# A fourth bank for picks, sums beside the constants, and pair steps two apart, in a graph edge kernel

## Chip, cores and metric

The kernel runs on one core of a Trainium2 chip. The metric is the device time of one execution, in microseconds (us). Engines are named as in the profile: PE (TensorE, matrix products), PEld (its weight loads), DVE (VectorE), ACT (ScalarE), POOL (GpSimd), SP (SyncE, here the queue that issues most transfers). PSUM is the memory that PE writes to; in this kernel it is cut into eight banks of 512 float32 numbers in each of 128 partitions.

## The reference

A layer of a graph network, 6250 nodes, 100000 edges and 128 features. For each edge the features of both ends and of the edge go through one matrix, a layer norm and a ReLU; the results are added up by source node; the node's own features are added and normalised.

```
msg_in = concatenate([x[row], x[col], edge_attr], axis=-1)   # 100000 x 384
h = msg_in @ W + b                                           # W: 384 x 128
mu, var = mean(h), mean(square(h - mu))                      # over 128 features
h = (h - mu) * rsqrt(var + 1e-5) * gamma + beta
msg = relu(h)
agg = segment_sum(msg, row, num_segments=6250)
out = layernorm(x + agg)                                     # eps 1e-5
```

Edges arrive sorted by `dst` (the column), not by `row`, so the sum over `row` needs a sort.

## The kernel before

**Three stages over the edges.** First the products of nodes with their part of W are made and cut into three bfloat16 terms (`project`, during the first split); those of the source nodes stay in SBUF as `xa`. Then a loop over 196 values of q takes four tiles of 128 edges at a time: `edge_loads` and `edge_window` fetch, `edge_hot` makes a one-hot matrix (DVE, L607), `edges` adds the edge's own product (PE, L619) and the destination node's row (PE, L623) in a bank `hp`, `evict` copies the bank out (ACT, L633), and `scatters` writes each row by an indirect transfer (POOL, L650) to its place in a table in DRAM, sorted by blocks of 125 source nodes. A row's place comes from `places`, a generator which for every piece of up to 44 tiles makes one-hots against an iota row (DVE, L451), runs a prefix sum (L455), counts (PE, L467 and L468; DVE, L470 to L472), multiplies (L474) and adds the 50 blocks up on PE (L502), a number `PG` of blocks side by side, which a reduction (DVE, L507) folds.

The tiles come in six splits, each with its own table. Once a split is written, its 25 pairs of blocks are worked on while the next split's edges go through the loop. That is the **pair stage**: 125 pairs of the first five splits, with eight tiles each (three splits), six or four. Pairs of eight or six tiles have two groups, of four or three tiles; pairs of four have one. The 25 pairs of the sixth split come in a tail, as 14 `Unit`s of one or two pairs, with their own lines (L847 to L958), among them sums (L912), which take turns between a bank `hp` and the bank of the sums.

**The steps of a pair** (class `Pair`), each in the program's order of its engine:

| step | engine, line | what it does |
|---|---|---|
| load | SP, L724 | a pair's rows from DRAM to `hl` |
| ones | DVE, L742 | one-hot of the row's node in its block, against the iota row in PSUM |
| turn, turned | PE, L754; ACT, L758 | transpose to a bank `tr`, copy out to `ohn` |
| seed(g) | ACT, L764 | rows of a group to a bank `sel` |
| pick(g) | PE, L781 | adds the source nodes' rows to them, three terms for each tile |
| square(g) | ACT, L790, L793 | sums of squares, standard deviation |
| root(g), scale(g) | DVE, L799, L805 | reciprocal, scaled and clipped row to `msg` |
| sums | PE, L814 | adds messages by node, in a bank `pa` |
| add | DVE, L819 | adds that to `acc` |

`FLOW` is a list of (step number, function), walked from the top once for each step of `work`; a pair starts a new round every four steps, so steps whose numbers are equal modulo four fall together, of pairs one or more apart. `due` and `steps_due` spread the steps over q: 100 steps over 42, 42, 30, 20 and 16 values of q, while the next split is written. One step comes between `edges` and `evict`, the others behind the scatters and the steps of `places`. From q = 13 on each q's scatters are tied to PE products through `done`.

**Banks before:** two `hp`, three `sel`, one `tr`, one `pa` and one `beside`. The last holds the iota row (`iota_p`, columns 0 to 127), a zero (`zero_p`), a piece's places so far (`at`), and from column 192 on `counts`: the counts, the 50 block sums of `places` (`PG` = 7 blocks of up to 44 columns), the flags' sum and, in the tail, the row `beta_p` that `stats` (L930) reads. The framework adds the waits between engines by the tiles and banks that the instructions touch.

Of the kernel before, what the change touches and what calls it, by code (L numbers as in the profile page):

```python
# [8 lines left out]
F32 = mybir.dt.float32  # L9
BF16 = mybir.dt.bfloat16  # L10
# [6 lines left out]
P = 128  # L17
D = 128
# [6 lines left out]
NB, BN = 50, 125  # L25
# [6 lines left out]
PIECES = 196  # L32
TABLE_FROM = [0, 13, 45, PIECES]
HALF = PIECES // 2
BANKS = {"hp": 2, "sel": 3, "tr": 1}


SPLITS = [(168, 4, 320, [12, 24, 44, 44, 44]),
# [7 lines left out]
BY_PE = 4  # L46
FN = 4

PG = 7
PG_AT = 192  # L50
XG = 4
ROW = 132
ACW = 130
# [31 lines left out]
def fast_path(ctx, tc, io, bad_d, found):  # L85
# [88 lines left out]
    iota_i = const.tile([P, P], I32, name="iota_i")  # L174
# [12 lines left out]
    beside, counts = beside_t[:, :PG_AT], beside_t[:, PG_AT:]  # L187
    iota_p, zero_p, at = beside[:, 0:P], beside[:, P:P + 1], beside[:, P + 8:P + 8 + NB]
# [10 lines left out]
    over_w = const.tile([P, 2], F32, name="over_w")  # L199

    def constants():
        nc.vector.tensor_copy(iota_p, iota_i)
# [48 lines left out]
    def signs():  # L251
        nc.vector.tensor_scalar(gamma_r, gamma_r, 0.0, 2.0, op0=ALU.is_ge, op1=ALU.mult)
        nc.vector.tensor_scalar(sgn_r, gamma_r, -1.0, None, op0=ALU.add)
        spread = psum.tile([P, 512], F32, name="pa")[:, :D]
        nc.tensor.matmul(spread, ones_h[0:1, :], sgn_r, start=True, stop=True)
        nc.scalar.copy(sgn, spread)

# [115 lines left out]
    n_banks = 0  # L373
# [5 lines left out]
    def project(g, k):  # L379
# [4 lines left out]
        t0 = g * XG  # L384
        m = XG if k == 1 else min(XG, NB - t0)
        xT = xT_of[g, k % 2]
        name = ("sel", "sel", "tr", "sel")[n_banks % 4]
# [340 lines left out]
    class Pair:  # L728
# [78 lines left out]

        def sums(self):
            k = self.k
            pa_t = psum.tile([P, 512], F32, name="pa")  # L810
            self.pa = pa_t[:, :2 * ACW].rearrange("p (h d) -> p h d", h=2)
            for h in range(2):
                for j in range(h, k, 2):
                    pe(nc.tensor.matmul(self.pa[:, h, :], self.ohe[:, j, :], self.msg[:, j, :],  # L814
                                        start=(j == h), stop=(j == k - 2 + h)), 4)
# [12 lines left out]
    class Unit:  # L828
# [73 lines left out]
        def sums(self, g):  # L902
            if (self.p0 + g) % 2:
                pa_t = psum.tile([P, PT, P], F32, name="hp", bufs=BANKS["hp"])
                pa = flat(pa_t)
            else:
                pa = psum.tile([P, 512], F32, name="pa")
# [91 lines left out]
    first, second = pieces[0][1], pieces[1][1]  # L999
# [72 lines left out]
    FLOW = [(14, second(lambda x: x.add())), (11, second(lambda x: (x.root(1), x.scale(1)))),  # L1072
            (13, single(lambda x: x.add())),
            (9, lambda x: (x.root(0), x.scale(0))), (13, second(lambda x: x.sums())),
            (8, second(lambda x: x.pick(1))), (6, second(lambda x: x.pick(0))),
            (5, single(lambda x: x.pick(0))),
            (7, second(lambda x: x.seed(1))), (5, second(lambda x: x.seed(0))),
            (3, single(lambda x: (x.turned(), x.seed(0)))),
            (9, second(lambda x: x.square(1))), (7, lambda x: x.square(0)),
            (4, second(lambda x: x.turned())), (2, lambda x: x.turn()),  # L1080
            (10, single(lambda x: x.sums())),
            (0, lambda x: x.ones()),
            (-6, None)]

# [428 lines left out]
```

## Time and profile before

| | |
|---|---|
| median of 3 runs | 1356.2 us (1353.18 to 1357.1) |
| the profiled execution's own time | 1355.95 us |
| its span in the trace | 1354.1 us |
| mean granted TensorE clock | 0.855 of full |
| busy: PE, PEld, DVE | 978.5, 869.8, 852.2 us |
| busy: ACT, POOL | 766.6, 799.0 us |

A row of the groups gives the line, engine, operation and tiles, count, then busy time and mean duration of one in ns, and at last the idle time just before them with the releasers. A row of the waits reads: engine and line that waited, what it waited for, us in total, times, longest. "issue" is time in which nothing that the profile shows was waited for; "remote" is a semaphore whose sender the profile can't tell. A row of the timeline gives start and duration in us.

### The profile page before, as it was taken

The numbers are of one execution on the slowest core, as the hardware profiler recorded it, in microseconds if no ns is written. First come the engines' busy times: TensorE is split into PE (matmuls) and PEld (weight loads), VectorE is DVE, ScalarE is ACT, GpSimd is POOL, SyncE is SP. The second block draws the span as 40 slices with busy tenths as digits, with TensorE's granted clock in tenths as the row PEclk, the third lists the DMA queues.
The fourth block names the chain that finished last, engine by engine and source line by source line (L and its number), as shares of the span: only waits on it lengthen the run. The fifth ranks groups of instructions, "written<-read, shape, count | busy, mean of one in ns | idle before, by whom it ended". The sixth has DMA issues, their size and how long they took to land. (4 is left out here: it accounts for less than half of the span.)

```text
span 1354.1 us, 27281 instructions
## 1 busy us (share of the span) xinstructions
PE 978.5 (72%) x8886; PEld 869.8 (64%) x8886; DVE 852.2 (63%) x2376; ACT 766.6 (57%) x2988; POOL 799.0 (59%) x830
## 2 busy tenths in 40 slices
PE   7555546365768777777877778778878787776895
PEld 5454535344757766676666767777778787665674
DVE  8572425514665666656575667678688877654797
ACT  4223322112656655565555567677779788755796
POOL 3656666666666665666566666656665556556054
PEclk9768687666888887888888798989999999988998
DMA  7857677445666654556756555666667655543332
GB/s 225 251 172 243 191 229 223 138 155 167 192 204 208 203 160 162 166 181 193 219 177 195 174 191 180 218 199 191 188 200 235 189 186 188 158 147 99 108 126 70
DMA packets 128050, 247.20 MB, mean 183 GB/s; under 512 B 47005, under 2 KB 61231, under 8 KB 127897
## 3 DMA queue, kind: packets, MB, share of 16 engines
q1 hardware_dynamic: 101924, 191.92, 46.8%
q0 software_dynamic: 25104, 53.05, 11.1%
q8 instruction: 71, 1.16, 0.4%
q14 instruction: 81, 0.66, 0.1%
q10 hardware_dynamic: 870, 0.40, 0.1%
HBM read 155.49 MB, written 89.80 MB: 181 GB/s over the span
## 5 line engine op out<-in xcount | busy, mean ns | idle before, releaser
L650 POOL DMA_INDIRECT sorted<-hs,place_i x782 | 760.6, 973 | 474.7 <-issue 179.7
L781 PE MATMUL sel<-xa,ohn 128*128 128x128 bf16 x2550 | 210.8, 232 | 134.7 <-issue 65.5
L790 ACT ACTIVATE sq<-sel 128x128 f32<-128x128 f32 x850 | 224.5, 281 | 140.4 <-remote 47.2
L619 PE MATMUL hp<-w,eT 128*128 128x128 f32 x1564 | 261.2, 316 | 32.4 <-issue 20.5
L814 PE MATMUL pa<-msg,ohe 128*128 128x130 f32 x1700 | 259.0, 307 | 30.0 <-DVE msg L805 14.9
L619 PEld LDWEIGHTS hp<-w,eT 128*128 128x128 f32 x1564 | 235.0, 226 | 67.2 <-issue 32.9
L781 PEld LDWEIGHTS <-ohn 128*128 128x128 bf16 x2550 | 175.0, 104 | 154.4 <-issue 136.1
L633 ACT COPY hs<-hp 128x512 f32<-128x512 f32 x196 | 114.2, 584 | 273.9 <-remote 98.5
L814 PEld LDWEIGHTS pa<-msg,ohe 128*128 128x128 f32 x1700 | 234.8, 216 | 41.5 <-issue 24.2
L805 DVE SCALAR_TENSOR_TENSOR msg<-sel,rstd,cut 128x128 f32<-128x128 f32 x850 | 240.7, 346 | 8.0
L790 ACT ACTIVATION_READ_ACCUMULATOR sq<-sel 128x1 f32 x850 | 179.8, 212 | 0.0
L819 DVE TENSOR_TENSOR acc<-acc,pa 128x260 f32<-128x260 f32 x125 | 52.9, 423 | 184.7 <-remote 72.8
L742 DVE TENSOR_TENSOR ohe<-hl,beside 128x1024 f32<-128x1024 f32 (+2 forms) x125 | 131.6, 1053 | 24.2 <-remote 7.6
L758 ACT COPY ohn<-tr 128x1024 bf16<-128x1024 bf16 (+2 forms) x125 | 109.6, 877 | 42.8 <-remote 19.2
L764 ACT COPY sel<-hl 128x512 f32<-128x512 f32 (+1 forms) x225 | 128.5, 571 | 2.0 <-DVE msg L805 2.0
L607 DVE TENSOR_SCALAR ohd<-db,part_w 128x512 bf16<-128x512 bf16 x192 | 68.6, 357 | 68.4 <-remote 36.8
L623 PE MATMUL hp<-win,ohd 126*128 126x128 bf16 x782 | 90.5, 238 | 15.9 <-issue 13.3
L799 DVE RECIPROCAL rstd<-std 128x4 f32<-128x4 f32 (+1 forms) x225 | 38.7, 172 | 90.3 <-ACT std L793 45.2
L754 PE MATMUL tr<-ident_h,ohe 128*128 128x128 bf16 x850 | 77.0, 229 | 21.9 <-issue 19.9
L623 PEld LDWEIGHTS <-ohd 126*128 126x128 bf16 x782 | 69.5, 109 | 23.3 <-issue 18.9
L754 PEld LDWEIGHTS <-ohe 128*128 128x128 bf16 x850 | 57.7, 103 | 29.9 <-issue 29.9
L793 ACT ACTIVATE std<-ss,eps 128x4 f32<-128x4 f32 (+1 forms) x225 | 67.1, 298 | 7.3
(198 smaller groups left out, 1018.9 us busy)
## 6 DMA issues: line engine op xcount, KB each, us to landing
eT<-in_eT SPq DMA_DIRECT2D x96, 512.0 KB
hl<-sorted SPq DMA_DIRECT2D x75, 528.0 KB
db<-drel_d SPq DMA_DIRECT2D x96, 256.0 KB
sorted<-empty SPq DMA_DIRECT2D x100, 198.0 KB
hl<-sorted SPq DMA_DIRECT2D x50, 264.0 KB
sorted<-hs,place_i POOLq DMA_INDIRECT x782
hl<-sorted SPq DMA_DIRECT2D x25, 396.0 KB
sorted<-empty SPq DMA_DIRECT2D x50, 132.0 KB
```

The costliest lines, as they stand in the source:

```text
L619: pe(nc.tensor.matmul(hp[:, j, :], eT[:, at], w[:, 2, :], start=j == 0, stop=False, skip_group_check=True), 4)
L623: pe(nc.tensor.matmul(hp[:, j, :], oh[:3 * WN, at], win[:3 * WN, :], start=False, stop=j == m - 1, skip_group_check=True))
L633: nc.scalar.copy(hs[:, :m, 0:D], hp[:, :m, :])
L650: i = nc.gpsimd.indirect_dma_start(out=sorted_d[s][:, :], out_offset=bass.IndirectOffsetOnAxis(ap=place_i[:parts, t:t + 1], axis=0), in_=h ...
L742: nc.vector.tensor_tensor(self.ohe[:, :k, :], self.hl[:, :k, D:D + 1].to_broadcast([P, k, P]), row_bc(iota_p, k), op=ALU.is_equal)
L754: pe(nc.tensor.transpose(tr[:, j, :], half[:, j0 + j, 1::2], ident_h))
L758: nc.scalar.copy(self.ohn[:, :self.k, :], self.tr[:, :self.k, :])
L764: nc.scalar.copy(self.sel[g][:, :m, :], self.hl[:, j0:j0 + m, 0:D])
L781: pe(nc.tensor.matmul(sel[:, j, :], self.ohn[:, j0 + j, :], xa[:, b, i * D:(i + 1) * D], start=False, stop=j == m - 1 and i == 2, skip_gro ...
L790: nc.scalar.activation(sq[:, j, :], self.sel[g][:, j, :], AF.Square, accum_out=ss[:, j:j + 1])
L805: nc.vector.scalar_tensor_tensor(self.msg[:, j0 + j, 0:D], self.sel[g][:, j, :], rstd[:, j:j + 1], cut, op0=ALU.mult, op1=ALU.max)
L814: pe(nc.tensor.matmul(self.pa[:, h, :], self.ohe[:, j, :], self.msg[:, j, :], start=(j == h), stop=(j == k - 2 + h)), 4)
```

## The change

`BANKS["sel"]` goes from 3 to 4. The bank `pa` is gone: the pair's sums, those of even pairs in the tail and the spread of signs at the start go to columns 252 to 511 of the bank `beside`, named `sums_p`. To make room there, the iota row is kept as bfloat16 in 64 columns (made through a bfloat16 tile `iota_h` in SBUF), `counts` begins at column 120 and has 132 columns, and `PG` goes from 7 to 3. The projections of the start take turns among five banks. In `FLOW`, for pairs with two groups, seeds go from 5 and 7 to 4 and 5, pick 1 from 8 to 7, squares from 7 and 9 to 8 and 9, scale 0 from 9 to 10, the add from 14 to 15; for pairs with one group, only the sums move, from 10 to 11.

```
--- before.py
+++ after.py
@@ -32,7 +32,7 @@
 PIECES = 196
 TABLE_FROM = [0, 13, 45, PIECES]
 HALF = PIECES // 2
-BANKS = {"hp": 2, "sel": 3, "tr": 1}
+BANKS = {"hp": 2, "sel": 4, "tr": 1}
 
 
 SPLITS = [(168, 4, 320, [12, 24, 44, 44, 44]),
@@ -46,8 +46,9 @@
 BY_PE = 4
 FN = 4
 
-PG = 7
-PG_AT = 192
+PG = 3
+PG_AT = 120
+PA_AT = 252
 XG = 4
 ROW = 132
 ACW = 130
@@ -184,8 +185,10 @@
     iota_row = const.tile([P, P], F32, name="iota_row")
 
     beside_t = psum.tile([P, 512], F32, name="beside")
-    beside, counts = beside_t[:, :PG_AT], beside_t[:, PG_AT:]
-    iota_p, zero_p, at = beside[:, 0:P], beside[:, P:P + 1], beside[:, P + 8:P + 8 + NB]
+    counts, sums_p = beside_t[:, PG_AT:PA_AT], beside_t[:, PA_AT:]
+    iota_w, zero_p, at = beside_t[:, 0:P // 2], beside_t[:, P // 2:P // 2 + 1], beside_t[:, 68:68 + NB]
+    iota_p = iota_w.bitcast(BF16)
+    iota_h = const.tile([P, P], BF16, name="iota_h")
     part = const.tile([P, 1], F32, name="part")
     before = const.tile([P, P], BF16, name="before")
     ident_h = const.tile([P, P], BF16, name="ident_h")
@@ -199,7 +202,8 @@
     over_w = const.tile([P, 2], F32, name="over_w")
 
     def constants():
-        nc.vector.tensor_copy(iota_p, iota_i)
+        nc.vector.tensor_copy(iota_h, iota_i)
+        nc.vector.tensor_copy(iota_w, iota_h.bitcast(F32))
         nc.vector.tensor_copy(iota_row, iota_i)
         nc.vector.tensor_copy(part, part_i)
         nc.vector.memset(zero_p, 0.0)
@@ -251,7 +255,7 @@
     def signs():
         nc.vector.tensor_scalar(gamma_r, gamma_r, 0.0, 2.0, op0=ALU.is_ge, op1=ALU.mult)
         nc.vector.tensor_scalar(sgn_r, gamma_r, -1.0, None, op0=ALU.add)
-        spread = psum.tile([P, 512], F32, name="pa")[:, :D]
+        spread = sums_p[:, :D]
         nc.tensor.matmul(spread, ones_h[0:1, :], sgn_r, start=True, stop=True)
         nc.scalar.copy(sgn, spread)
 
@@ -384,7 +388,7 @@
         t0 = g * XG
         m = XG if k == 1 else min(XG, NB - t0)
         xT = xT_of[g, k % 2]
-        name = ("sel", "sel", "tr", "sel")[n_banks % 4]
+        name = ("sel", "sel", "tr", "sel", "sel")[n_banks % 5]
         n_banks += 1
         ps = psum.tile([P, XG, P], F32, name=name, bufs=BANKS[name])
         for j in range(m):
@@ -807,8 +811,7 @@
 
         def sums(self):
             k = self.k
-            pa_t = psum.tile([P, 512], F32, name="pa")
-            self.pa = pa_t[:, :2 * ACW].rearrange("p (h d) -> p h d", h=2)
+            self.pa = sums_p.rearrange("p (h d) -> p h d", h=2)
             for h in range(2):
                 for j in range(h, k, 2):
                     pe(nc.tensor.matmul(self.pa[:, h, :], self.ohe[:, j, :], self.msg[:, j, :],
@@ -904,7 +907,7 @@
                 pa_t = psum.tile([P, PT, P], F32, name="hp", bufs=BANKS["hp"])
                 pa = flat(pa_t)
             else:
-                pa = psum.tile([P, 512], F32, name="pa")
+                pa = sums_p
             pa = pa[:, :2 * ACW].rearrange("p (h d) -> p h d", h=2)
             for h in range(2):
                 for j in range(h, self.kp, 2):
@@ -1069,16 +1072,18 @@
     def single(step):
         return lambda x: step(x) if len(x.groups) == 1 else None
 
-    FLOW = [(14, second(lambda x: x.add())), (11, second(lambda x: (x.root(1), x.scale(1)))),
+    FLOW = [(15, second(lambda x: x.add())), (11, second(lambda x: (x.root(1), x.scale(1)))),
             (13, single(lambda x: x.add())),
-            (9, lambda x: (x.root(0), x.scale(0))), (13, second(lambda x: x.sums())),
-            (8, second(lambda x: x.pick(1))), (6, second(lambda x: x.pick(0))),
+            (9, single(lambda x: (x.root(0), x.scale(0)))),
+            (10, second(lambda x: (x.root(0), x.scale(0)))), (13, second(lambda x: x.sums())),
+            (7, second(lambda x: x.pick(1))), (6, second(lambda x: x.pick(0))),
             (5, single(lambda x: x.pick(0))),
-            (7, second(lambda x: x.seed(1))), (5, second(lambda x: x.seed(0))),
+            (5, second(lambda x: x.seed(1))), (4, second(lambda x: x.seed(0))),
             (3, single(lambda x: (x.turned(), x.seed(0)))),
-            (9, second(lambda x: x.square(1))), (7, lambda x: x.square(0)),
+            (9, second(lambda x: x.square(1))), (8, second(lambda x: x.square(0))),
+            (7, single(lambda x: x.square(0))),
             (4, second(lambda x: x.turned())), (2, lambda x: x.turn()),
-            (10, single(lambda x: x.sums())),
+            (11, single(lambda x: x.sums())),
             (0, lambda x: x.ones()),
             (-6, None)]
```

More of the change, by code (lines that the diff above doesn't have):

```diff
@@ L34 @@
 HALF = PIECES // 2
-BANKS = {"hp": 2, "sel": 3, "tr": 1}
+BANKS = {"hp": 2, "sel": 4, "tr": 1}
 SPLITS = [(168, 4, 320, [12, 24, 44, 44, 44]),
@@ L47 @@
 FN = 4
-PG = 7
-PG_AT = 192
+PG = 3
+PG_AT = 120
+PA_AT = 252
 XG = 4
@@ L186, in fast_path @@
     beside_t = psum.tile([P, 512], F32, name="beside")
-    beside, counts = beside_t[:, :PG_AT], beside_t[:, PG_AT:]
-    iota_p, zero_p, at = beside[:, 0:P], beside[:, P:P + 1], beside[:, P + 8:P + 8 + NB]
+    counts, sums_p = beside_t[:, PG_AT:PA_AT], beside_t[:, PA_AT:]
+    iota_w, zero_p, at = beside_t[:, 0:P // 2], beside_t[:, P // 2:P // 2 + 1], beside_t[:, 68:68 + NB]
+    iota_p = iota_w.bitcast(BF16)
+    iota_h = const.tile([P, P], BF16, name="iota_h")
     part = const.tile([P, 1], F32, name="part")
@@ L253, in signs @@
         nc.vector.tensor_scalar(sgn_r, gamma_r, -1.0, None, op0=ALU.add)
[L254 removed]
+        spread = sums_p[:, :D]
         nc.tensor.matmul(spread, ones_h[0:1, :], sgn_r, start=True, stop=True)
@@ L386, in project @@
         xT = xT_of[g, k % 2]
-        name = ("sel", "sel", "tr", "sel")[n_banks % 4]
+        name = ("sel", "sel", "tr", "sel", "sel")[n_banks % 5]
         n_banks += 1
@@ L1070, in single @@
         return lambda x: step(x) if len(x.groups) == 1 else None
-    FLOW = [(14, second(lambda x: x.add())), (11, second(lambda x: (x.root(1), x.scale(1)))),
+    FLOW = [(15, second(lambda x: x.add())), (11, second(lambda x: (x.root(1), x.scale(1)))),
             (13, single(lambda x: x.add())),
-            (9, lambda x: (x.root(0), x.scale(0))), (13, second(lambda x: x.sums())),
-            (8, second(lambda x: x.pick(1))), (6, second(lambda x: x.pick(0))),
+            (9, single(lambda x: (x.root(0), x.scale(0)))),
+            (10, second(lambda x: (x.root(0), x.scale(0)))), (13, second(lambda x: x.sums())),
+            (7, second(lambda x: x.pick(1))), (6, second(lambda x: x.pick(0))),
             (5, single(lambda x: x.pick(0))),
-            (7, second(lambda x: x.seed(1))), (5, second(lambda x: x.seed(0))),
+            (5, second(lambda x: x.seed(1))), (4, second(lambda x: x.seed(0))),
             (3, single(lambda x: (x.turned(), x.seed(0)))),
-            (9, second(lambda x: x.square(1))), (7, lambda x: x.square(0)),
+            (9, second(lambda x: x.square(1))), (8, second(lambda x: x.square(0))),
+            (7, single(lambda x: x.square(0))),
             (4, second(lambda x: x.turned())), (2, lambda x: x.turn()),
-            (10, single(lambda x: x.sums())),
+            (11, single(lambda x: x.sums())),
             (0, lambda x: x.ones()),
```

8 lines of the change are left out of this document (4 added, 4 removed).

## The prediction

> **What bounds the kernel now.** I read the page first, then the busy times by stage, then the waits by stage, then the rows of the lines the change touches, and last the timeline of single pairs. The pair stage runs from 307 us (first one-hot matrix, L742) to 1262 us; where one split's pairs give way to the next (830, 1021, 1152 us) I cut it into A (50 pairs of eight tiles), B (25 of eight), C (25 of six) and D (25 of four). A tail follows.
>
> ```profile
> span 1354.1 us, 27281 instructions
> PE 978.5 (72%) x8886; PEld 869.8 (64%) x8886; DVE 852.2 (63%) x2376; ACT 766.6 (57%) x2988; POOL 799.0 (59%) x830
> ...
> 307.00:830.00 523.00, 392.15 (x3535) 350.43 (x3535) 317.29 (x822) 295.25 (x1141) 327.21 (x338) 0.84 0.59 186
> 830.00:1021.00 191.00, 152.43 (x1646) 144.16 (x1644) 144.26 (x398) 142.66 (x581) 114.93 (x119) 0.94 0.63 201
> 1021.00:1152.00 131.00, 106.79 (x1195) 101.77 (x1194) 101.61 (x308) 109.01 (x459) 76.32 (x79) 0.96 0.62 194
> 1152.00:1262.00 110.00, 77.32 (x755) 71.35 (x751) 58.81 (x186) 68.75 (x292) 57.33 (x59) 0.86 0.43 129
> ```
>
> Behind each window stand its length and the busy times of PE, weight load, DVE, ACT and POOL. No engine is full. PE is busy 75% of A, 80% of B and 82% of C, and idles 131, 38.6 and 24.2 us there. Four engines hand each pair round, every one of them in its program's order, so hand-overs set the pace. Those that hold PE and ACT, over the whole span:
>
> ```profile
> ACT sq L790 <- remote: 47.2, 19, 4.9
> PE sel L781 <- ACT sel L764: 48.1, 45, 3.8
> ACT sq L790 <- PE sel L781: 38.2, 22, 6.4
> ACT sel L764 <- DVE msg L805: 2.0, 5, 1.0
> ```
>
> The pick (L781) waited 45 times, 48.1 us in all, for the seed (L764), one step ahead of it; the square (L790) waited 38.2 us for the pick, also one step ahead. The last row says that three sel banks delayed the seeds by only 2.0 us. By stage, A, then B and C together, then D:
>
> ```profile
> PE sel L781 <- ACT sel L764: 11.3, 12, 3.2
> PE sel L781 <- issue: 45.5, 66, 2.8
> PE pa L814 <- DVE msg L805: 0.3, 1, 0.3
> ...
> PE sel L781 <- ACT sel L764: 25.7, 24, 3.1
> ...
> PE sel L781 <- ACT sel L764: 11.1, 9, 3.8
> ```
>
> In A the picks lose most to "issue", which no spacing of steps touches. The sums (L814) wait for next to nothing in A (0.3 us), and in B and C no such wait shows at all: that is a free slot which the change spends.
>
> **The spacing: the gain.** For pairs with two groups seed to pick and pick to square become two steps where they were one; square to scale stays two; the sums stay at 13 and the add goes from 14 to 15. Single-group pairs (D) have seed to pick at two steps already, so D's 11.1 us stay. At stake on PE are A's 11.3 and the 25.7 of B and C: 37 us. I take all of it, for a seed has another 1.9 us or more (B: 191/25/4 us a step; C: 1.3) and most waits were shorter: 25.7/24 is 1.1 us. The squares' 38.2 us lie on ACT; they delay what is queued there (eviction, seed, the copy L758), and reach the end only through these. I count a quarter, 10 us; bounds are nothing and all 38. So −47, between −37 and −75. The fourth sel bank pays for the seed's earlier place: its buffer now lives six steps and comes round every eight, before four and six. The slack is two steps as before, so the 2.0 us stay and this costs nothing. Each step takes only its own instructions along: none of the moved steps issues a DMA, and the load (step −6, SP), the ones (step 0), the turn and the scatters (POOL) keep their places. PE's order within a cycle of four steps stays sums, pick 0, turn, pick 1; DVE's stays add, scale 1, ones, scale 0.
>
> ACT's order does change: from turned, seed 0, square 1, seed 1, square 0 spread over the cycle to seed 0, square 0, turned in one step and seed 1, square 1 in the next. Turned now stands behind four squares, and pick 0 of the same pair, two steps on, needs it.
>
> ```profile
> L758 ACT COPY ohn<-tr 128x768 bf16<-128x768 bf16 x25 | 19.7, 788 | 2.9 <-PE pa L814 2.2 <-PE sel L781 0.4 <-PE hp L623 0.2
> L764 ACT COPY sel<-hl 128x384 f32<-128x384 f32 x50 | 24.2, 485 | 0.7 <-DVE msg L805 0.7
> 878.98 0.29 ACT L790 ACTIVATE sq<-sel 128x128 f32<-128x128 f32 x1
> ...
> 879.24 0.29 ACT L790 ACTIVATE sq<-sel 128x128 f32<-128x128 f32 x1
> ...
> L793 ACT ACTIVATE std<-ss,eps 128x4 f32<-128x4 f32 (+1 forms) x225 | 67.1, 298 | 7.3
> ```
>
> In C that is a seed 0.49, three squares 0.26 apart (879.24 less 878.98), std 0.30 and turned 0.79: 2.3 us against two steps of 1.3. It just fits. I add 2 us (bounds 0 and 25, one microsecond per pair of C).
>
> **The shared bank: the cost.** The sums leave their own bank for the one with the iota row, zero, the slot counts and the place sums. Do two engines have to keep apart there, though their columns differ? In the kernel before, the ones read the iota (columns 0 to 127) while L502 writes from column 192 on, and yet:
>
> ```profile
> L742 DVE TENSOR_TENSOR ohe<-hl,beside x125: 671/1210/1223, 307.4 to 1262.5; 128x1024 f32<-128x1024 f32 x75, 128x768 f32<-128x768 f32 x25, 128x512 f32<-128x512 f32 x25
> ...
>   PE beside L502: 6.0, 3
> ...
> who waited for it (us, times):
>   PE beside L502: 0.6, 1
> ```
>
> Each waited for the other: the bank is ordered as a whole, and since each engine keeps its program's order, everything behind the waiting instruction waits too. [...] If columns alone counted, this whole part would be nil.
>
> So the sums wait for the last DVE access of the bank that the program puts ahead of them, and the DVE accesses behind them wait for the sums' end. In A, B and C the one ahead is mostly the ones of the pair three further on, which come in the step before. Two pairs of B, as they ran:
>
> ```profile
> 876.85 1.22 DVE L742 TENSOR_TENSOR ohe<-hl,beside 128x1024 f32<-128x1024 f32 x1
> 877.45 2.00 PE L814 MATMUL pa<-msg,ohe 128*128 128x130 f32 x16
> 877.98 2.23 DVE L455 TENSOR_TENSOR_SCAN sc<-oh,beside 128x1000 f16<-128x1000 bf16 x1
> ...
> 883.20 2.29 DVE L455 TENSOR_TENSOR_SCAN sc<-oh,sc,beside 128x1000 f16<-128x1000 bf16 x1
> 883.32 1.84 PE L814 MATMUL pa<-msg,ohe 128*128 128x130 f32 x15
> 885.40 1.20 DVE L742 TENSOR_TENSOR ohe<-hl,beside 128x1024 f32<-128x1024 f32 x1
> ```
>
> In both the scan comes ahead of the sums in the new program, in the second the ones too. The first sums could then start at 877.98 + 2.23 = 880.21, 2.8 us late; the second (first matmul at 883.12) at 886.60, 3.5 us late. Taken in this way pair by pair, the lateness adds up to 39.7 us in A, 38.1 in B (18 of 25 pairs late) and 24.5 in C (22 of 25): 102 us. It cannot all land: a sum pushed back gives the next DVE access time to be done before it, and it pushes picks that had idled behind it anyway. Nor can it be free: PE's busy time plus this lateness is 152.4 + 38.1 = 190.5 us in B (191 now) and 106.8 + 24.5 = 131.3 in C (131 now), so the new waits fill all the idle time that PE has, and the stages end where they were only if every other wait is gone. I take half, +51, between a quarter (26) and all.
>
> In D the sums are never late, but the ones follow them in the program and now lose their cover: 0.68 us that today runs beside the sums comes between sums and add.
>
> ```profile
> 1179.85 1.13 DVE L805 SCALAR_TENSOR_TENSOR msg<-sel,rstd,cut 128x128 f32<-128x128 f32 x4
> 1180.34 2.09 PE L814 MATMUL pa<-msg,ohe 128*128 128x130 f32 x8 [1.05 <-DVE msg L805]
> 1180.89 0.68 DVE L742 TENSOR_TENSOR ohe<-hl,beside 128x512 f32<-128x512 f32 x1
> ```
>
> DVE is busy 58.8 of D's 110 us, so most of 25 × 0.68 = 17 us finds room: +2, bounds 0 and 17. In the tail, sums of even pairs share the bank with its own one-hot step; startup gains one copy: together +1 (0 to 4).
>
> **Groups of three: the rest of the layout.** To make room, a group's place sums shrink from seven terms to three: per pass 17 matmuls of up to 126 columns instead of 8 of up to 308.
>
> ```profile
> 974.75 1.02 PE L502 MATMUL beside<-sc,ident_f 128*128 128x280 f16 x8
> ...
> 879.29 0.83 PE L781 MATMUL sel<-xa,ohn 128*128 128x128 bf16 x12
> ...
> L507 DVE TENSOR_REDUCE pos<-beside 128x40 f32<-128x280 f32 x5 | 2.2, 442 | 0.0
> L451 DVE TENSOR_TENSOR oh<-bkt_h,beside x38: 774/1241/1394, 7.2 to 1052.2; 128x1050 bf16<-128x1050 bf16 x16, 128x1000 bf16<-128x1000 bf16 x10, 128x1100 bf16<-128x1100 bf16 x6, 128x975 bf16<-128x975 bf16 x4
> ```
>
> By the pick's row a matmul of 128 columns costs 0.069 us, so 17 are 1.17 against 1.02: 0.15 more, over some 19 pieces of three passes +8 us of PE, of which the part before 307 us and the gaps hide half: +4. The reduce (L507) reads under half as much, at most 0.3 us less in each of 19: −2 with the other DVE time hidden. The iota becomes bf16, so L451's inputs are both of two bytes; at 1.24 us for 1050 elements nothing shows that it would speed up (one of them is a broadcast), and I take 0; were it to halve, 38 × 0.62 = 24 us of DVE would go, some 8 on the path. [...]
>
> **The sum:** −47 + 2 + 51 + 2 + 1 + 4 − 2 = +11 us, on the profiled execution's 1355.95 (span 1354.1): 1367. That execution stands 0.25 us below the median of 1356.2, so the median goes to 1367 too.
>
> **Rivals.** *Decoupling wins* (faster). The waits of pick and square go and the ones, given a step's notice, are mostly done when the sums come: a quarter of the lateness lands (26), the gains reach −60 and the small terms stay +7: −27, 1329. For it: ACT and PE wait in turn for each other in one-step distances. Against: A, the longest stage, has only 11.3 us of pick-on-seed waits, and 12 of 19 ones that stand last before the sums in B end after the sums' present start. It decides where less than two fifths of the 102 us land (47 − 7 = 40).
>
> *The bank becomes the loop* (much slower). Sums wait for DVE's ones and scans, DVE's next bank access waits for the sums, and each round carries lateness to the next. Nine tenths of the 102 land, gains stay at −37, D costs its 17, the rest +5: +77, 1433; with three quarters (+76) and D at 8, +52, 1408.
>
> *It doesn't do what it says* (same). The fourth bank is eaten by the longer life, the seeds were no cause (late for ACT's backlog, which stays), and bank waits only move idle time: within 4 us of 1356.
>
> **How the numbers follow.** A measurement of this kernel tells about 0.3% (4 us) from no change. Forecast, a little slower (1360 to 1395): 0.42; the bank as the loop: 0.15; same: 0.10; decoupling wins: 0.33. Slower is 0.57, same 0.10, faster 0.33. The range takes in the faster rival's middle and the lower part of the slower one: 1324 to 1405; the likeliest case's own is 1360 to 1395.
>
> **What would show it.** Right: picks waiting for seeds fall under 12 us outside D; new rows "L814 waits for ohe L742" and for L455, L451, L474, together 30 to 70 us; rows of ones and scans waiting for the sums, 10 to 40 us; in D the ones start only as the sums end. PE's busy time rises by 5 to 10 us, L507 falls under 0.3 us. Wrong: L814's waits for DVE under 25 us (then faster), or stage A shorter by over 10 us; or B and C both longer by over 25 us (the loop).

## The result, and the profile after

The changed kernel took 1441.67 us (median of 6 runs, 1436.3 to 1448.38) beside 1357.29 us for the kernel before: 1.0635 times as long, 95% interval 1.0612 to 1.0658. That is 84 us more, where the prediction said 11 more and a range up to 1405. The sign was right, the size was not. The profiled execution took 1436.3 us, with a span of 1434.5, 80.4 us more than before.

The page of the changed kernel, its totals; then its windows by stage, cut where the ones (now L746) of the next split begin, with the start and the tail (length, then busy PE, PEld, DVE, ACT, POOL):

```profile
span 1434.5 us, 28299 instructions
PE 986.3 (69%) x9391; PEld 898.7 (63%) x9391; DVE 850.9 (59%) x2377; ACT 765.5 (53%) x2988; POOL 798.0 (56%) x830
...
0.00:317.00 317.00, 172.17 (x1208) 147.79 (x1209) 151.97 (x358) 78.50 (x150) 187.52 (x203) 0.71 0.65 195
317.00:865.00 548.00, 384.10 (x3752) 361.27 (x3751) 314.74 (x820) 294.74 (x1145) 324.97 (x335) 0.84 0.57 178
865.00:1081.00 216.00, 158.86 (x1701) 150.99 (x1700) 143.62 (x400) 140.33 (x566) 114.94 (x120) 0.90 0.58 180
1081.00:1229.00 148.00, 113.14 (x1279) 107.47 (x1279) 101.73 (x307) 111.01 (x469) 77.18 (x80) 0.94 0.56 168
1229.00:1335.00 106.00, 80.45 (x762) 72.28 (x760) 59.65 (x189) 69.41 (x297) 57.10 (x59) 0.89 0.45 135
1335.00:1434.00 99.00, 77.60 (x702) 58.85 (x698) 79.15 (x310) 71.49 (x367) 36.32 (x35) 0.95 0.30 96
```

Against the windows of before: the start +10 us, A +25, B +25, C +17, D −4, the tail +7. Every engine's share falls while its work stays: PE is busy 8 us more in all, DVE, ACT and POOL no more than before. All but these 8 of the 80 us are idle time of PE. The 10 us at the start come ahead of any pair's sums, so they are not made by sums and DVE waiting for each other; there PE's idle time ahead of the place products (L502, now L506) that is put to "issue" went from 2.4 to 35.8 us. Where PE idles is told by the groups of PE lines, first of before (which the prediction did not show for the sums), then of after:

```profile
L781 PE MATMUL sel<-xa,ohn 128*128 128x128 bf16 x2550 | 210.8, 232 | 134.7 <-issue 65.5 <-ACT sel L764 48.1 <-ACT sc L477 11.3
L814 PE MATMUL pa<-msg,ohe 128*128 128x130 f32 x1700 | 259.0, 307 | 30.0 <-DVE msg L805 14.9 <-issue 14.6
```

```profile
L785 PE MATMUL sel<-xa,ohn 128*128 128x128 bf16 x2550 | 200.5, 230 | 60.6 <-ACT ohn L762 24.6 <-issue 20.0 <-ACT sel L768 15.3
L817 PE MATMUL beside<-msg,ohe 128*128 128x130 f32 x1700 | 285.9, 330 | 158.8 <-DVE ohe L746 47.8 <-issue 41.7 <-DVE oh L455 28.8
```

The picks' idle time went from 134.7 to 60.6 us; ahead of the sums it went from 30.0 to 158.8, and ahead of the place products from 16.3 to 59.4. Of the picks' 74 us, 32.8 are waits for seeds (48.1 to 15.3), which the change means to remove. Another 45.5 are "issue" (65.5 to 20.0), and these only moved: over all lines of PE the list of waits puts 188 us to "issue" before and 182 after. What grew in all is waits with a name. What the sums, DVE and ACT wait for, from that list of the changed kernel:

```profile
DVE acc L822 <- PE beside L817: 56.1, 33, 4.8
PE beside L817 <- DVE ohe L746: 47.8, 29, 4.3
ACT sq L794 <- PE sel L785: 35.6, 19, 7.8
ACT sel L768 <- DVE msg L809: 31.8, 12, 5.5
PE beside L817 <- DVE oh L455: 28.8, 9, 5.7
DVE ohe L746 <- PE beside L817: 22.8, 19, 2.2
PE beside L817 <- DVE far L478: 21.7, 9, 4.3
DVE sc L459 <- PE beside L817: 11.3, 5, 2.8
DVE beside L474 <- PE beside L817: 9.5, 4, 3.7
PE beside L817 <- DVE sc L459: 7.9, 3, 3.3
```

Four rows of 47.8, 28.8, 21.7 and 7.9, with 0.3 from L511 below them, make 106.5 us in which PE stands ahead of the sums for a DVE access of the bank: 46.5 in A, 34.2 in B, 25.0 in C and 0.8 in D. In the other direction DVE's accesses of the bank behind the sums, the add apart, waited 54.5 us in all (22.8, 11.3 and 9.5 here, 10.9 for L511, L478 and L850 below); the add itself waited 56.1 us, 44.2 before. The seeds, too, now wait for the scales that free their banks: 31.8 us, 2.0 before. The timeline shows how it goes, in B:

```profile
1056.67 2.18 DVE L459 TENSOR_TENSOR_SCAN sc<-oh,beside 128x975 f16<-128x975 bf16 x1
1058.76 1.19 DVE L746 TENSOR_TENSOR ohe<-hl,beside 128x1024 f32<-128x1024 f32 x1
1060.01 2.05 PE L817 MATMUL beside<-msg,ohe 128*128 128x130 f32 x16 [2.01 <-DVE ohe L746]
...
1066.96 1.21 DVE L746 TENSOR_TENSOR ohe<-hl,beside 128x1024 f32<-128x1024 f32 x1
1068.22 2.05 PE L817 MATMUL beside<-msg,ohe 128*128 128x130 f32 x16 [3.25 <-DVE ohe L746]
...
1074.19 1.21 DVE L746 TENSOR_TENSOR ohe<-hl,beside 128x1024 f32<-128x1024 f32 x1
1075.45 2.57 PE L817 MATMUL beside<-msg,ohe 128*128 128x130 f32 x16 [2.22 <-issue]
```

Scan, ones, sums: each begins as the one before it ends, on two engines that ran side by side before (in B, ones from 876.85 to 878.07 us, sums from 877.45 us). The last row is a lesson in reading: its 2.22 us are put down to "issue", yet the sums begin 0.05 us after the ones end (1074.19 + 1.21 = 1075.40), just as in the two rows above. So part of the 41.7 us of "issue" ahead of the sums is the bank as well; of the rise of 128.8 us, 106.5 are named.

### The profile page after: what moved, and what is told of

Its sections match the earlier page's. It is cut to its first block, busy times and chain, and to the rows that moved or that the text cites. A ratio compares the mean times of both kernels' runs of the same rounds, so it can differ in the third digit from the quotient of the medians.

```text
span 1434.5 us, 28299 instructions
## 1 busy us (share of the span) xinstructions
PE 986.3 (69%) x9391; PEld 898.7 (63%) x9391; DVE 850.9 (59%) x2377; ACT 765.5 (53%) x2988; POOL 798.0 (56%) x830
## 5 line engine op out<-in xcount | busy, mean ns | idle before, releaser
L817 PE MATMUL beside<-msg,ohe 128*128 128x130 f32 x1700 | 285.9, 330 | 158.8 <-DVE ohe L746 47.8
L817 PEld LDWEIGHTS beside<-msg,ohe 128*128 128x128 f32 x1700 | 256.4, 235 | 179.8 <-DVE ohe L746 53.2
L623 PE MATMUL hp<-w,eT 128*128 128x128 f32 x1564 | 247.5, 307 | 13.9 <-issue 13.2
L623 PEld LDWEIGHTS hp<-w,eT 128*128 128x128 f32 x1564 | 226.3, 219 | 46.4 <-issue 31.4
L794 ACT ACTIVATE sq<-sel 128x128 f32<-128x128 f32 x850 | 224.3, 282 | 55.5 <-PE sel L785 35.6
L785 PE MATMUL sel<-xa,ohn 128*128 128x128 bf16 x2550 | 200.5, 230 | 60.6 <-ACT ohn L762 24.6
L785 PEld LDWEIGHTS <-ohn 128*128 128x128 bf16 x2550 | 169.8, 104 | 69.5 <-ACT ohn L762 34.5
L746 DVE TENSOR_TENSOR ohe<-hl,beside 128x1024 f32<-128x1024 f32 (+2 forms) x125 | 131.6, 1052 | 45.4 <-PE beside L817 22.8
L768 ACT COPY sel<-hl 128x512 f32<-128x512 f32 (+1 forms) x225 | 128.1, 570 | 42.9 <-DVE msg L809 31.8
L822 DVE TENSOR_TENSOR acc<-acc,beside 128x260 f32<-128x260 f32 x125 | 52.4, 419 | 137.5 <-PE beside L817 56.1
L762 ACT COPY ohn<-tr 128x1024 bf16<-128x1024 bf16 (+2 forms) x125 | 108.9, 871 | 32.8 <-remote 10.3
L627 PE MATMUL hp<-win,ohd 126*128 126x128 bf16 x782 | 83.6, 232 | 6.1 <-issue 3.7
L758 PEld LDWEIGHTS <-ohe 128*128 128x128 bf16 x850 | 57.6, 103 | 15.9 <-issue 14.3
```

Of the source, the lines that this page charges most:

```text
L623: pe(nc.tensor.matmul(hp[:, j, :], eT[:, at], w[:, 2, :], start=j == 0, stop=False, skip_group_check=True), 4)
L627: pe(nc.tensor.matmul(hp[:, j, :], oh[:3 * WN, at], win[:3 * WN, :], start=False, stop=j == m - 1, skip_group_check=True))
L746: nc.vector.tensor_tensor(self.ohe[:, :k, :], self.hl[:, :k, D:D + 1].to_broadcast([P, k, P]), row_bc(iota_p, k), op=ALU.is_equal)
L758: pe(nc.tensor.transpose(tr[:, j, :], half[:, j0 + j, 1::2], ident_h))
L762: nc.scalar.copy(self.ohn[:, :self.k, :], self.tr[:, :self.k, :])
L768: nc.scalar.copy(self.sel[g][:, :m, :], self.hl[:, j0:j0 + m, 0:D])
```

## The experiments

Each ratio is to runs of the kernel before in the same session. The sessions differ: the kernel before took 1357.3 us in the one of the result, 1371.0, 1355.3 and 1372.0 in three others, and 1119.7 and 1121.8 in two more. I call them long and short sessions and compare within a kind. More on this at the end.

| kernel | session | ratio | 95% interval |
|---|---|---|---|
| the change (three times) | long | 1.0635, 1.0646, 1.0588 | 1.0612–1.0658, 1.0575–1.0717, 1.0525–1.0651 |
| change with old steps (twice) | long | 1.0430, 1.0441 | 1.0364–1.0495, 1.0387–1.0495 |
| change, constants in SBUF | long | 1.0263 | 1.0212–1.0314 |
| before, groups of three | long | 1.0172 | 1.0122–1.0222 |
| before, constants in SBUF | long | 1.0105 | 1.0071–1.0140 |
| change, turned first | long | 1.0678 | 1.0618–1.0738 |
| change, ones a step earlier | long | 1.0561 | 1.0505–1.0617 |
| before, seeds a step earlier | long | 0.9997 | 0.9975–1.0020 |
| before, new steps, own bank (twice) | short | 1.0561, 1.0551 | 1.0546–1.0576, 1.0535–1.0567 |
| change, ones a step earlier | short | 1.0794 | 1.0756–1.0832 |
| change, constants in SBUF | short | 1.1036 | 1.1015–1.1058 |
| the same with old steps (twice) | short | 1.1059, 1.1050 | 1.1036–1.1083, 1.1033–1.1066 |
| before, larger groups | short | 0.9998 | 0.9989–1.0007 |

**Constants out of the bank, and old steps.** Theories: the shared bank; the new steps by themselves; the groups of three.

```
-    iota_w, zero_p, at = beside_t[:, 0:P // 2], ..., beside_t[:, 68:68 + NB]
-    iota_p = iota_w.bitcast(BF16)
+    zero_p = const.tile([P, 1], F32, name="zero_p")
+    at = const.tile([P, NB], F32, name="at")
     iota_h = const.tile([P, P], BF16, name="iota_h")
+    iota_p = iota_h
```

> The changed kernel with the iota row (bfloat16), the zero and a piece's places kept in SBUF tiles; the bank beside then holds only the counts, the place sums and the pairs' sums. Bank theory (the loss is sums and DVE's reads of the constants waiting for each other): most of the 84 us goes, 1345 to 1385 us, and PE's idle time ahead of the sums falls from 158.8 us to under 60. Spacing theory (the new step numbers bunch ACT's work, and that costs): stays above 1420 us, idle ahead of the sums little changed. Groups theory (17 short products a pass instead of 8): stays above 1420 us too.

1.0263 (1408.78 us), with PE's idle time ahead of the sums down to 62.4:

```profile
L817 PE MATMUL beside<-msg,ohe 128*128 128x130 f32 x1700 | 277.0, 311 | 62.4 <-issue 30.9 <-DVE msg L809 12.8 <-DVE acc L822 11.1
```

The waits for the ones, the scans and the multiplication are gone from ahead of the sums; 2.9 us for other place steps (L511, L475) are left. More than half of the loss went with the DVE accesses; the bank theory is right in kind, though not all of what it expected came back, because groups of three and the reads from SBUF cost more than thought, as the next ones show.

For the old steps the `FLOW` list of before stands in the changed kernel, for example

```
-            (5, second(lambda x: x.seed(1))), (4, second(lambda x: x.seed(0))),
+            (7, second(lambda x: x.seed(1))), (5, second(lambda x: x.seed(0))),
...
-    FLOW = [(15, second(lambda x: x.add())), ...
+    FLOW = [(14, second(lambda x: x.add())), ...
```

> The changed kernel with the step numbers of before; shared bank, four sel banks and groups of three stay. Bank theory: as slow as the change or slower, 1430 to 1470 us, with PE waiting for both the bank and the seeds. Spacing theory: back to 1355 to 1375 us.

> The changed kernel with the old step numbers, again beside the change on its own chip. Bank theory: shared bank and groups of three make most of the loss, so 1.035 to 1.06. Spacing theory: below 1.025.

1.0430 and 1.0441: slower than before and faster than the change. With the old steps the bank is shared just as much, but the sums wait less for it:

```profile
L817 PE MATMUL beside<-msg,ohe 128*128 128x130 f32 x1700 | 281.1, 327 | 117.7 <-issue 45.4 <-DVE ohe L746 42.9 <-DVE far L478 7.2
L785 PE MATMUL sel<-xa,ohn 128*128 128x128 bf16 x2550 | 202.8, 230 | 93.2 <-ACT sel L768 52.8 <-issue 32.3 <-ACT ohn L762 3.5
```

PE stood ahead of the sums for DVE's bank accesses 62.6 us where the change has 106.5 (63.1 and 104.0 in the session that ran both), and DVE's accesses, the add apart, 24.6 where it has 54.5. The add's own wait for the sums is longer, 83.2 against 56.1, so DVE in all waits for the sums as much as in the change; the difference is on PE. The picks wait for seeds again (52.8 us against 15.3), and yet in the session that ran both the kernel is 2.0% faster than the change (1.0646 / 1.0441). So the new steps, on this bank, cost 24 us by the medians and 28 by the ratios. That they line the ones, the place steps and the sums up worse is what PE's waits say; why they do (in the old list scale 0 stands in the sums' own step and gives DVE something to do meanwhile) is argued only.

**Groups of three alone.** In the kernel before:

```
-PG = 7
+PG = 3
```

> The kernel before with PG = 3 instead of 7, nothing else. Bank and spacing theories: 1355 to 1365 us (the prediction's +4 -2). Groups theory: 1380 us or more.

1.0172, about 24 us: just short of the 1380 us of the groups theory (1.018), and ten times what the prediction's terms came to (+4 − 2). The product's group by its three weights, before and then with three, with the first form's name in each row:

```profile
L502 PE MATMUL beside<-sc,ident_f 128*128 128x294 f16 (+7 forms) x152 | 25.2, 314 | 4.2 <-issue 3.6 <-DVE ohe L742 0.6
L502 PE MATMUL beside<-sc,minus_f 128*128 128x294 f16 (+10 forms) x144 | 23.9, 304 | 5.8 <-issue 5.8
L502 PE MATMUL beside<-far,twice_f 128*128 128x294 f16 (+7 forms) x144 | 23.9, 306 | 6.3 <-issue 6.2
```

```profile
L502 PE MATMUL beside<-sc,minus_f 128*128 128x126 f16 (+10 forms) x306 | 31.4, 247 | 18.9 <-issue 18.5
L502 PE MATMUL beside<-far,twice_f 128*128 128x126 f16 (+7 forms) x306 | 28.9, 252 | 11.4 <-issue 11.3
L502 PE MATMUL beside<-sc,ident_f 128*128 128x126 f16 (+6 forms) x323 | 27.5, 244 | 10.4 <-issue 8.9 <-DVE ohe L742 1.2
```

Busy 73.0 to 87.8 us, idle ahead of them 16.3 to 40.7, nearly all of it "issue", with 935 products where there were 440. The two traces are from different sessions; the kernel before with its constants in SBUF (below), with groups of seven in the session of the second trace, has 70.4 and 21.9. That the products meet more of PE's stalls is the reading at hand, but it is not shown: over all lines of PE, "issue" comes to 203 us with groups of three and to 226 in that other kernel, so the idle time may have moved to this line rather than been added. The price of 24 us is measured, its cause is open. In short sessions the same three groups were busy 60.5 us in the kernel before and 62.3 with groups of three (in the changed kernel with constants in SBUF and old steps), and idle 3.1 and 0: there the products take even less than the 8 us more that I had worked out. Groups of three alone were not run in a short session.

**Fewer products than before.** In the kernel before, the iota row as in the change, and the freed columns to the place sums, 8 to 10 blocks in the later pieces:

```
-PG = 7
-PG_AT = 192
+PG_AT = 120
...
+            PG = min((512 - PG_AT) // T, NB)
```

> The kernel before with the iota row as bfloat16 in 64 columns of the bank and the freed columns given to the place sums: 8 to 10 blocks side by side instead of 7, so 5 to 7 products a pass instead of 8; the sums keep their own bank, the steps are the old ones. If the price of a product is what groups of three show (1.7% for 27 more a pass), 0.1 to 0.2% faster; 0.994 to 1.002 in all. If the smaller count frees more than that: below 0.994.

0.9998, in a short session, where by the rows above the number of products costs almost nothing. It does not tell what it would do in a long one.

**The control for constants in SBUF.** In the kernel before, the three constants become SBUF tiles:

```
-    iota_p, zero_p, at = beside[:, 0:P], beside[:, P:P + 1], beside[:, P + 8:P + 8 + NB]
+    iota_p = const.tile([P, P], BF16, name="iota_p")
+    zero_p = const.tile([P, 1], F32, name="zero_p")
+    at = const.tile([P, NB], F32, name="at")
```

> The kernel before with the iota row (bfloat16), the zero and a piece's places in SBUF tiles, as a control for x1: does it cost DVE anything to read them there? If it costs nothing: 1350 to 1358 us, ones 1.21 us as before. If DVE's reads from SBUF are slower or held up by POOL: ones or place steps longer by a tenth or more and 1365 us or more.

1.0105. The ones took 1.055 us on average (1.053 before), as the first alternative had it, but POOL paid, which neither alternative foresaw. The scatters, before and here:

```profile
L650 POOL DMA_INDIRECT sorted<-hs,place_i x782 | 760.6, 973 | 474.7 <-issue 179.7 <-PE pa L814 67.1 <-remote 50.6
```

```profile
L652 POOL DMA_INDIRECT sorted<-hs,place_i x782 | 868.2, 1110 | 393.5 <-issue 198.1 <-PE pa L816 47.2 <-remote 35.4
```

It is the place and not the type of the iota row: the changed kernel, with a bfloat16 row in PSUM, has 0.971 us a scatter. So x1 carries the groups' price and this one: if the two multiply, 1.0172 × 1.0105 = 1.0279, and it measured 1.0263. The three intervals together leave some 11 us either way, so the 47 us of the spacing are not there; a small gain or loss could be.

**The spacing by itself.** The kernel with constants in SBUF, with new and with old steps, side by side:

> The changed kernel with the constants in SBUF and the new step numbers (the kernel of x1), beside the next one on the same chip. If the spacing is worth what the prediction gave it (47 us) it is 3% faster than the next one; if it is worth nothing, within 0.8% of it; if it costs by itself, slower by over 0.8%.

> The changed kernel with the constants in SBUF and the old step numbers. See the run before: 3% slower than it if the spacing gains, equal if it is worth nothing. On a chip of the slower kind, by the prices so far (1.017 for the groups times 1.010 for the constants in SBUF), 1.02 to 1.035 of before if the spacing is worth nothing.

> The changed kernel with the constants in SBUF (as x1) and the old step numbers. Against x1 (1.026 of before) it prices the spacing where the bank is shared only with the place steps. If the spacing gains when the bank is nearly free: 1.035 or more. If it costs by itself: 1.015 or less.

1.1036 and 1.1050 in one session, 1.1059 in the other short one: worth nothing here. (The last ran in a short session, so it can't be set beside x1's 1.0263 as its expectation meant to.) PE's wait at the picks changes its name and is 35 us shorter with the new steps, and the time does not follow; new steps first, old steps second:

```profile
L785 PE MATMUL sel<-xa,ohn 128*128 128x128 bf16 x2550 | 199.6, 233 | 129.8 <-ACT ohn L762 98.9 <-ACT sel L768 30.4
```

```profile
L785 PE MATMUL sel<-xa,ohn 128*128 128x128 bf16 x2550 | 195.2, 230 | 164.6 <-ACT sel L768 164.1
```

With the old steps the picks wait for the seeds, with the new ones for the copy of the transposes, which ACT now has behind four squares. That these kernels are so slow in short sessions has, it seems, another reason: POOL is busy 922 of x5's 1237 us, a scatter taking 1.130 us. So the comparison is one under a load on POOL; new and old steps with the constants in SBUF were not run side by side in a long session.

The new steps alone in the kernel before, with the sums in their own bank and three sel banks:

> The kernel before with the new step numbers alone: the sums keep their own bank, groups of seven, three sel banks, so that a sel buffer now lives six steps of the six in which it comes round. Bank theory with the prediction's view of the spacing: the picks' waits for seeds fall, seeds wait for scales instead, 0.985 to 1.01 of before. Spacing theory (the new order of ACT's work costs by itself): 1.015 or more.

> The kernel before with the new step numbers alone (the kernel of x6, which lost 5.6% on the chip of the faster kind), three sel banks. Seeds then wait for scales, since a buffer lives as long as it takes to come round. If this chip is of the slower kind, where PE loses time to issue, a part of that is covered: 1.01 to 1.04 of before. If the price is the same everywhere: 1.05 to 1.06.

1.0561 and 1.0551, both in short sessions. The seeds of before (traced again in the first short session, 0.9998) and with new steps:

> The kernel before, unchanged, for a trace on the chip that runs the others: the ratio is 1, within 0.5%.

```profile
L764 ACT COPY sel<-hl 128x512 f32<-128x512 f32 (+1 forms) x225 | 128.1, 570 | 15.8 <-DVE msg L805 15.4 <-issue 0.2
```

```profile
L764 ACT COPY sel<-hl 128x512 f32<-128x512 f32 (+1 forms) x225 | 127.7, 567 | 148.7 <-DVE msg L805 147.0 <-DMA hl<-sorted 1.4
L781 PE MATMUL sel<-xa,ohn 128*128 128x128 bf16 x2550 | 190.8, 227 | 134.1 <-ACT ohn L758 97.9 <-ACT sel L764 34.8 <-issue 0.4
```

Without the fourth bank the seeds wait 147.0 us for scales, with four banks (and constants in SBUF) 15.2: the fourth bank is what the steps need. And the picks wait 97.9 us for the copy (none of the 104.3 us they idle in the kernel before in that session is put down to it). No run had the new steps, four sel banks and the sums in a bank of their own with the constants in PSUM: that is nine banks, one more than these kernels have.

A smaller dose, in the kernel before, both seeds one step earlier:

```
-            (7, second(lambda x: x.seed(1))), (5, second(lambda x: x.seed(0))),
+            (6, second(lambda x: x.seed(1))), (4, second(lambda x: x.seed(0))),
```

> The kernel before with both seeds one step earlier (5 to 4, 7 to 6) and nothing else; a sel buffer then lives five steps of six. If picks really lose what they wait for seeds (48.1 us on PE in the first trace of before, 103.3 us on the faster chip): 0.97 to 0.99 of before. If seeds then wait for scales or ACT's order costs as much: 0.995 to 1.02.

0.9997. The waits of picks for seeds fell from 48.1 to 31.1 us, those for the copy rose from 3.9 to 10.0, the picks' idle time fell from 134.7 to 109.4, and the time did not move. What picks wait for seeds is not what the kernel could gain.

**Two tries at the rest of the loss.** The copy put ahead of the seeds and squares again, in the changed kernel:

```
+            (4, second(lambda x: x.turned())),
             (5, second(lambda x: x.seed(1))), (4, second(lambda x: x.seed(0))),
...
-            (4, second(lambda x: x.turned())), (2, lambda x: x.turn()),
+            (2, lambda x: x.turn()),
```

> The changed kernel with the copy of the transposes (turned) put ahead of seed 0 and square 0 in its step, so that ACT does it first, as it did before. If pick 0 waiting for that copy (24.6 us on PE in the changed kernel's first trace) is a price of its own: 1 to 2.5% faster than the change, and that wait under 8 us. If the sums' wait for the bank sets the pace: within 0.7% of the change.

1.0678 beside 1.0646: no gain. The picks' wait for the copy fell from 21.8 to 5.6 us (the change in that session, and this), the sums' wait for DVE's bank accesses went from 104.0 to 110.7 and their "issue" from 45.2 to 70.2. But the 21.8 us hold little that the new place of the copy could give back: 16.6 are one wait at the first picks of the pair stage, and it is still there, 14.3 us, now put to "issue". In the first trace of the change the same wait is 15.6 of 24.6 us, and ACT stands then not at squares but at an eviction:

```profile
334.63 0.59 ACT L637 COPY hs<-hp 128x512 f32<-128x512 f32 x1 [15.61 <-remote]
...
336.70 1.46 PE L785 MATMUL sel<-xa,ohn 128*128 128x128 bf16 x12 [15.56 <-ACT ohn L762]
```

Groups of three alone and the old steps have a wait of 11 to 12 us at this place, too.

The ones a step earlier, so two steps ahead of the sums:

```
-            (0, lambda x: x.ones()),
+            (-1, lambda x: x.ones()),
```

> The changed kernel with the ones at step -1 instead of 0, so two steps ahead of the sums that wait for them, after the add. Bank theory: PE's wait for the ones ahead of the sums (47.8 us in the changed kernel) falls by more than half and the time by 20 to 45 us, to 1.03 to 1.05 of before. If that wait only stands in for others: within 0.7% of the change, 1.056 to 1.07.

> The changed kernel with the ones a step earlier (the kernel of x7). If the wait for the ones is what the sums lose: 1.5 to 3.5% faster than the change beside it. If one bank access of DVE only takes the place of another: within 0.7%.

> The changed kernel, for comparison with the next. On a chip of the slower kind 1.064 again. On one of the faster kind, where nothing covers a wait and groups of three cost nothing by the rows of the product's line (62.3 us busy against 60.5), 1.06 to 1.10 from the bank alone.

> The changed kernel, unchanged, beside the next three on one chip, since the chips that ran the earlier studies differ (the kernel before took 1371 us on one and 1120 us on another). If its loss is made of waits that any chip has, 1.05 to 1.08 of before on either kind.

1.0561 beside 1.0588 in one long session: the same within what the runs can tell. Rows of the change in that session and, below, of the kernel with the ones a step earlier:

```profile
PE beside L817 <- DVE ohe L746: 54.4, 30, 6.5
PE beside L817 <- DVE oh L455: 28.2, 8, 5.7
PE beside L817 <- DVE far L478: 19.3, 7, 4.5
```

```profile
PE beside L817 <- DVE ohe L746: 33.9, 17, 4.5
PE beside L817 <- DVE far L478: 30.4, 12, 5.0
PE beside L817 <- DVE oh L455: 24.6, 8, 5.1
```

The ones give back 20 us and the multiplication of places (L478) takes 11 of them; PE's idle time ahead of the sums only goes from 156.3 to 147.4. It is not one badly placed instruction: whichever access of DVE comes last before the sums, they wait for it. In the short session the same kernel is 1.0794 of before, beyond both alternatives of its expectation, which took the session for a long one. PE's list of waits puts 2 us to "issue" there, so the price of bank and steps together is not tied to the stalls of long sessions.

## Why the prediction went wrong

Its sum was −47 (spacing) + 2 (turned) + 51 (bank) + 2 (D) + 1 (tail) + 4 − 2 (groups) = +11. Measured in long sessions, as far as parts can be told apart: groups 24, shared bank with the old steps 35, the new steps on that bank 24 to 28, together 83 to 87 where the whole is 84 us by the medians and 86 by the ratio.

- **The spacing, −47: the step that failed most.** I counted the picks' waits for seeds in A, B and C (37 us) as time that PE gets back, all of it, and a quarter of the squares' waits. The picks' waits for seeds did go, outside D to the last one, and the time did not follow. The squares' waits for the picks did not even go: 35.6 us beside 38.2. And the fourth bank, "this costs nothing", left seeds waiting 31.8 us for scales where the prediction kept 2.0. A wait removed on an engine that is busy 75 to 82% of the time is not a gain until one knows what is late next, and here ACT's copy, the "issue" stalls or the bank were. Seeds a step earlier: 0.9997. New steps with the bank nearly free: 1.0263 measured where the prices of groups and SBUF multiplied give 1.0279, and 1.1036 beside 1.1050 with the old steps. On the shared bank they cost 2.0%, 24 to 28 us. The step's own sentence "I take all of it" was the mistake.
- **The shared bank, +51: right in kind, and near in size.** With the old steps it costs 1.0430 / 1.0172 = 1.025 in one session, some 35 us (with a fourth sel bank that the old steps don't need); with the new ones 1.0646 / 1.0172 = 1.047 across sessions, some 63 us, in which what the new steps cost is counted again. The lateness read off the timeline of before, 39.7, 38.1 and 24.5 us in A, B and C, came out as 46.5, 34.2 and 25.0 us of PE's waits by name. So the reason given for the halving did not hold: the waits were not halved by DVE being done in time, most likely because DVE is held back by the same bank (54.5 us besides the add). That only some 0.6 of them reached the end (63 of 106) made the half a fair guess all the same, and that is luck. The rival in which the bank becomes the loop, 1408 to 1433 us at a chance of 0.15, came nearest and still fell short; its lateness landed, but the gains of −37 that it kept were not there, and the groups cost more.
- **Groups of three, +2: mis-sized.** 24 us. I priced 17 products from a row without stalls and hid half of them, the part ahead of 307 us among it; the change's start alone is 10 us longer, with 35.8 us of "issue" ahead of these products. Whether more products meet more stalls, or what else makes the 24 us, no run tells.
- **D, +2, and the tail, +1.** In D the ones do wait for the sums (19 times, 22.8 us) as said, and D is 4 us shorter all the same: no price shows. The tail is 7 us longer, outside the bounds of 0 to 4 that were to hold the start as well: its sums wait 6.1 us for the ones, and its adds on the shared bank 10.2 us for the sums (2.9 before).
- **Turned behind the squares, +2.** Of the 24.6 us that picks wait for the copy, 15.6 are the one wait behind an eviction; in C, where the term was placed, 5.8 us in four waits are left. To put the copy first gained nothing.
- **iota in bfloat16, 0:** right. L451's steps take 1.218 us on average (now L455), 1.219 before.

Of the marks named in advance, the sums' waits for DVE were to be 30 to 70 us and were 106.5, and the ones and scans waiting for sums 10 to 40 us: 34.1. PE's busy time rose by 8 us and L507 (now L511) fell to 0.28 us, both as named. Picks waiting for seeds were to fall under 12 us outside D: all of the 15.3 us that are left stand in D. B is 25 us longer, C 17: short of the mark for the loop by a little.

## What to carry to other kernels

Giving a producer's sums a bank that another engine reads for constants tied the two engines here, though sums and constants have columns of their own: PE waited 106.5 us for DVE's accesses ahead of the sums, and DVE's accesses, the add apart, 54.5 us for the sums. So count the accesses by engine and order, not the columns; the lateness read off the trace of before, 102 us, came out in full as waits. A wait in the profile is a gain only after one small run has shown that removing it moves the end; here one with the seeds a step earlier would have told it before the layout was rebuilt. More and shorter instructions may cost more than their durations in a clean row say (here 24 us for 8), so a part of a change that looks free is worth a run by itself. And before a fall of one line's idle time is called a gain, add the cause up over all lines: "issue" only moved.

## What the runs showed of the hardware

The same kernel took 1355 to 1372 us in four sessions and 1120 to 1122 in two. In the short one that was traced with the kernel before, no wait is put down to "remote", PE's picks have no "issue" idle time (65.5 us in the first trace), and the granted clock is 0.914 against 0.855. Every trace of a short session has some 2 us of PE's time (weight loads apart) put to "issue" in all, those of long sessions 161 to 272. Some expectations above speak of chips of a faster and a slower kind; but the record has the same chip number, 5, for two of the long sessions and a short one, so the number alone does not tell the kind. What makes it, and what stalls PE in the long ones, is open. It changes which term weighs: reading the constants from SBUF goes with a loss of 1% in a long session, and in short ones the kernels that do so are the slowest of those run.

The scatters' instruction on POOL got slower when DVE read its constants from SBUF instead of PSUM, 0.973 to 1.110 us in 782 of them (0.968 with groups of three alone, in the session of the second), while DVE's own instructions kept their times: the ones 1.053 and 1.055 us, the places' one-hots (L451, now L453) 1.219 and 1.221, their multiplication (L474, now L476) 1.223 and 1.228. In all five traces with the constants in SBUF a scatter takes 1.110 to 1.138 us. Why, no run shows. In a long session the constants' place in PSUM is worth 1.0%, some 14 us.
